# Block maxima and scales of the media for two tiles at once in the first sweep of a gated cross-attention stack

## The chip, the cores and the metric

The kernel runs on one core of one Trainium2 chip. The metric is the device time of one execution in microseconds (us), the median over the runs. A core has five engines that run their own instruction streams and wait for each other through semaphores: TensorE (PE in the profile, its weight loads PEld), VectorE (DVE), ScalarE (ACT), GpSimd (POOL) and SyncE (SP, which here issues the DMAs).

## The reference

Four gated residual layers over x of shape (4, 1024, 1024), with a second input of the same shape, the media (`ctx_2048`). The first layer is the one that the change touches:

```python
def quant_dequant_act_1x128(x):
    E, M, K = x.shape
    xb = x.reshape(E, M, K // BLK, BLK)
    amax = jnp.max(jnp.abs(xb), axis=-1, keepdims=True)
    safe = jnp.maximum(amax, ACT_EPS)
    q = (xb * (FP8_MAX / safe)).astype(jnp.float8_e4m3fn)
    return (q.astype(jnp.float32) * (safe / FP8_MAX)).reshape(E, M, K)

def quant_dequant_weight_128x128(w):
    E, N, K = w.shape
    wb = w.reshape(E, N // BLK, BLK, K // BLK, BLK)
    amax = jnp.max(jnp.abs(wb), axis=(2, 4), keepdims=True)
    safe = jnp.maximum(amax, W_EPS)
    q = (wb * (FP8_MAX / safe)).astype(jnp.float8_e4m3fn)
    return (q.astype(jnp.float32) * (safe / FP8_MAX)).reshape(E, N, K)

xq = quant_dequant_act_1x128(x)
wq = quant_dequant_weight_128x128(weight)
return jnp.einsum('emk,enk->emn', xq, wq)
...
x = x + jnp.tanh(g_xattn[0]) * _L0_xattn_ref(_layernorm(x, axis=-1), ctx_2048)
x = x + jnp.tanh(g_ffn[0]) * _L0_ffn_ref(_layernorm(x, axis=-1), L0_ffn_weight, L0_ffn_norm_weight)
x = x + jnp.tanh(g_xattn[1]) * _L1_xattn_ref(_layernorm(x, axis=-1), ctx_2048, ctx_2048)
x = x + jnp.tanh(g_ffn[1]) * _L1_ffn_ref(_layernorm(x, axis=-1), L1_ffn_router_w, L1_ffn_Wa, L1_ffn_Wb)
```

The media of one batch are the weight matrix of the first layer. They are scaled in blocks of 128 x 128 by the largest magnitude of each block, rounded to the grid of an 8-bit float, and scaled back. The other three layers are a ternary linear layer, an attention over the media with 8 heads, and a mixture of 8 low-rank experts, 2 per token.

## The kernel before

The 4096 rows are 32 tiles of 128 rows (`NT` = 32), 8 to a batch (`TPB`). The **first sweep** (to about 555 us) computes the first layer, writes the sum `x1` to DRAM and gathers what the second layer needs of it. A **second sweep** (to about 1670 us) does the second and third layer and the routing, and a last part runs the experts.

In the first sweep there are two kinds of tiles. A `Rows` tile t holds 128 rows of x. A `Media` tile t holds 128 channels of the media, which are 128 x 1024 numbers: eight blocks of 128 columns side by side. All eight media tiles of a batch make its weight matrix, kept in two halves of 512 outputs (`wqs`, four buffers).

For a media tile these methods run, one after the other, in several steps of the sweep:

- `load` (L253): SP fetches the tile `c` (four buffers).
- `range` (L257): DVE reduces the magnitudes of each block over its columns, 128 x 1024 to 128 x 8 (`rmax`), and PE transposes this to 8 x 128 in PSUM (`rmaxT`).
- `largest` (L266): DVE takes the largest along each of the 8 rows (`top`), puts the eight values on the diagonal of an 8 x 8 matrix (`spot`), and PE multiplies a matrix of ones by it, so that each partition gets all eight block maxima (`bmax`, 128 x 8 in PSUM). One such product in float32 is two passes on PE in the profile.
- `scales` (L276): DVE computes `safe`, its reciprocal, `up` and, for tiles that are not scaled on ACT, `lift`; POOL computes `down`. All are 128 x 8.
- `magnitude` (L289): ACT writes the magnitudes in bfloat16.
- `round` (L296): DVE rounds to the 8-bit grid, with eight operations on 128 x 128 for `k16` (L203), eight for `y` (L208) and one subtraction (L213). In the opening, even tiles are scaled on ACT first (`scale`, L293).
- `store` (L302): ACT and DVE scale back into `wqs`, four blocks each (L237, L241), or seven and one for the first batch.

A `Rows` tile goes through `sum`, `mean`, `square`, `variance`, `range`, `scales`, `scale`, `round`, `restore` (`hd`, L237), `transpose` (eight `ptx` on PE, L375), `take` (`hT`, L381) and `product(0)`, `product(1)` (L388, eight float32 matmuls for each half, which are sixteen rows of the profile), then `residual` (L397), which writes `x1`, `spread`, `factor` and, for some tiles, `extreme` (L426).

The order on PE, DVE, ACT and POOL is the order in which the program is written (`tc.manual_schedule`, L588). SP's order is not written by hand. An **opening** (L589 to L652) prepares the first batch's media, two tiles in each of four rounds, and the first rows. Then `step(t)` (L517) runs for t = 0 to 31. Step t works on several tiles at different depths: `product` of row t, `restore` and `transpose` of row t+1, `scales` and `round` of row t+2, and of the media `store` of tile t+7, `scales` and `round` of tile t+8, `range`, `largest` and `magnitude` of tile t+9, `load` of tile t+11. Media tiles end at 31, so that `largest` runs in steps 0 to 22. In a step PE's order is `product(0)`, `rmaxT`, eight `ptx`, `product(1)`, `bmax`. DVE's is the row scales' reciprocal, the shared part of `store`, `residual` of row t-1, media `range`, media `scales` and `round`, `factor` and `extreme` of row t-2 (even t only, up to step 26), `variance` and `range` of row t+3, `round` of row t+2, and media `top` and `spot`.

The transposed maxima and the spread ones share two PSUM buffers (`ps_r`). From step 23 on, reloads of `x1` and the ternary weights of the second layer are worked in beside the products.

Of the kernel before, what the change touches and what calls it, by code (L numbers as in the profile page):

```python
# [53 lines left out]
def flamingo_kernel(  # L54
# [106 lines left out]
    def cols(k):  # L161
        return slice(k * P, (k + 1) * P)


    with ExitStack() as s1:
# [5 lines left out]

        gamma_2 = wb_sb[:, 6, :]

        ones_8 = w1.tile([NB, P], F32, tag="ones_8", name="ones_8", bufs=1)
        nc.gpsimd.memset(ones_8, 1.0)


        wqs = {}
# [66 lines left out]
        class Media(Fp8):  # L245


            def __init__(self, t):
                self.t, self.name = t, f"w{t}"

                self.scaled = t < TPB and t % 2 == 0
# [3 lines left out]
                nc.sync.dma_start(self.c, vr[self.t])  # L255

            def range(self):  # L257
                rmax = self.tiny("rmax")
                nc.vector.tensor_reduce(
                    rmax, self.c.rearrange("p (b k) -> p b k", k=P), AX.X, ALU.max,  # L260
                    apply_absolute_value=True,
                )
                self.turned = ps_r.tile([NB, P], F32, tag="r", name=f"rmaxT_{self.t}")
                nc.tensor.transpose(self.turned, rmax, ident)

            def largest(self):  # L266


                top = small.tile([NB, 1], F32, tag="topw", name=f"top_{self.name}")
                nc.vector.tensor_reduce(top, self.turned, AX.X, ALU.max)  # L270
                spot = small.tile([NB, NB], F32, tag="spot", name=f"spot_{self.name}")
                nc.vector.tensor_scalar(spot, ident[0:NB, 0:NB], top, None, ALU.mult)
                self.amax = ps_r.tile([P, NB], F32, tag="r", name=f"bmax_{self.t}")
                nc.tensor.matmul(self.amax, ones_8, spot, start=True, stop=True)

            def scales(self):  # L276

                safe = self.tiny("safe")
                nc.vector.tensor_scalar(safe, self.amax, W_EPS, None, ALU.max)
                self.up = self.tiny("up")  # L280
                nc.vector.reciprocal(self.up, safe)
                nc.vector.tensor_scalar(self.up, self.up, FP8_MAX, None, ALU.mult)
                if not self.scaled:
                    self.lift = self.tiny("lift")
                    nc.vector.tensor_scalar(self.lift, self.up, FP8_LIFT, None, ALU.mult)
                self.down = self.tiny("down")
                nc.gpsimd.tensor_scalar(self.down, safe, 1.0 / FP8_MAX, None, ALU.mult)

            def magnitude(self):  # L289
                self.size = w1.tile([P, D], BF16, tag="sizew", name=f"size_{self.name}")  # L290
# [11 lines left out]
            def store(self):  # L302
                b, hf, j = self.t // TPB, self.t % TPB // NH, self.t % NH
                if (b, hf) not in wqs:
                    wqs[b, hf] = wqp.tile([P, NB, HALF], F32, tag="wq", name=f"wq_{b}_{hf}")
                self.dequantize(wqs[b, hf][:, :, cols(j)], 4 if b else 1)

        class Rows(Fp8):

# [171 lines left out]
        rows = [Rows(t) for t in range(NT)]  # L481
        media_t = [Media(t) for t in range(NT)]

        def at(items, t):
            return items[t] if 0 <= t < len(items) else None

# [30 lines left out]
        def step(t):  # L517

            near, new, ahead, far, past, old = (at(rows, t + i) for i in (1, 2, 3, 4, -1, -2))
            mp, m, mr, mn = (at(media_t, t + TPB + i) for i in (-1, 0, 1, 3))
            last = t - (NT - TPB)
            if ahead:
                ahead.mean()
            if new:
                new.scales()
            if t:
                rows[t].product(0)
            if near:  # L530
                near.restore()
            if mp and t:
                mp.store()
            if ahead:
                ahead.square()
            if past:
                past.residual()
            if mr:
                mr.range()
            if new:  # L540
                new.scale()
            if near:
                near.transpose()
                near.take()
            if m:
                m.scales()
                m.round()
            if old:
                old.factor()
                if old not in waiting:  # L550
                    old.extreme()
            if ahead:
                ahead.variance()
                ahead.range()
            if new:
                new.round()
            rows[t].product(1)
            if mr:
                mr.largest()
            if past:  # L560
                past.spread()
            if mr:
                mr.magnitude()
            if far:
                far.sum()
            if at(rows, t + 5):
                rows[t + 5].load()
            if mn:
                mn.load()
            if last >= 0:  # L570
                for r in waiting[2 * last : 2 * last + 2]:
                    r.late_extreme()
            if last >= -1:
                for r in waiting[2 * last + 2 : 2 * last + 4]:
                    r.reload()

            if last in (0, 1):
                load_linear(last)
            if 1 <= last < 5:
                ternary_sum(2 * last - 2)  # L580
                ternary_sum(2 * last - 1)
            if last == 4:
                ternary_scale()
            if 5 <= last:
                for j in range(3 * (last - 5), min(3 * (last - 4), NB)):
                    ternary_block(j)

        with tc.manual_schedule(engines=ORDERED):  # L588
            media_t[0].load()  # L589
            rows[0].load()  # L590
            for i in (1, 2, 3):
                media_t[i].load()
            for r in rows[1:5]:
                r.load()
            media_t[0].range()
            rows[0].sum()
            rows[0].mean()
            rows[0].square()
            media_t[1].range()
            for m in media_t[0:2]:  # L600
                m.largest()
                m.scales()
            media_t[1].magnitude()
            media_t[0].scale()
            rows[0].variance()
            rows[0].range()
            for i in range(TPB // 2):
                m, n = media_t[2 * i : 2 * i + 2]
                nexts = media_t[2 * i + 2 : min(2 * i + 4, TPB + 1)]
                n.round()  # L610
                if i == 0:
                    rows[0].scales()
                    rows[0].scale()
                elif i == 1:
                    rows[1].sum()
                elif i == 2:
                    rows[1].scales()
                    rows[1].scale()
                else:
                    rows[2].sum()  # L620
                n.store()
                nexts[-1].magnitude()
                for j in nexts:
                    j.range()
                if i in (1, 3):
                    rows[(i + 1) // 2].mean()
                    rows[(i + 1) // 2].square()
                m.round()
                m.store()
                for j in range(2 * i + 4, min(2 * i + 6, TPB + 3)):  # L630
                    media_t[j].load()
                for j in nexts:
                    j.largest()
                if i < 3:
                    for j in nexts:
                        j.scales()
                    nexts[0].scale()
                if i == 0:
                    rows[0].round()
                    rows[0].restore()  # L640
                    rows[0].transpose()
                    rows[0].take()
                elif i == 1:
                    rows[1].variance()
                    rows[1].range()
                    rows[0].product(0)
                elif i == 2:
                    rows[1].round()
                else:
                    rows[2].variance()  # L650
                    rows[2].range()
                    rows[3].sum()  # L652
            constants()
            for t in range(NT):
                step(t)
                if t == 3:
                    clear()
            rows[NT - 2].factor()
            rows[NT - 2].extreme()
            first_scale()  # L660
            rows[NT - 1].residual()
            rows[NT - 1].spread()
            rows[NT - 1].factor()
            rows[NT - 1].extreme()
# [988 lines left out]
```

## Time and profile before

| | |
|---|---|
| runs | 2026.25, 2027.53, 2030.4 us; median 2027.53 |
| the profiled execution | 2027.54 us; its span 2025.3 us; mean granted clock of TensorE 0.989 |
| first sweep, steps 1 to 22 (84.63 to 419.67 us) | PE busy 335.04 of 335.04 us, DVE 308.39, ACT 289.25, POOL 127.02 |
| `rmax`, 128 x 8 from 128 x 1024, DVE L259 | 32 times, median 1.209 us |
| `rmaxT`, 128 x 8 transposed, PE L264 | 32 times, median 0.273 us |
| `top`, DVE L270 | 32 times, median 0.272 us |
| `spot`, DVE L272 | 32 times, median 0.219 us |
| `bmax`, PE L274 | 64 passes for 32 products, median 0.272 us |
| `safe`, reciprocal, `up`, `lift`, DVE L279 to L285 | 32, 32, 32 and 28 times, medians 0.156, 0.203, 0.171 and 0.172 us |
| `down`, POOL L287 | 32 times, median 0.233 us |
| media load, SP L255 | 32 times 512 KB, median 3.7 us to landing |

Durations of neighbouring instructions overlap on every engine: from the start of one to the start of the next is often less than its duration. The matmuls' rows above show 0.27 us, though PE starts another one after about 0.11 us.

### The profile page before, as it was taken

The numbers are of one execution on the slowest core, as the hardware profiler recorded it, in microseconds if no ns is written. First come the engines' busy times: TensorE is split into PE (matmuls) and PEld (weight loads), VectorE is DVE, ScalarE is ACT, GpSimd is POOL, SyncE is SP. The second block draws the span as 40 slices with busy tenths as digits, with TensorE's granted clock in tenths as the row PEclk, the third lists the DMA queues.
The fourth block names the chain that finished last, engine by engine and source line by source line (L and its number), as shares of the span: only waits on it lengthen the run. The fifth ranks groups of instructions, "written<-read, shape, count | busy, mean of one in ns | idle before, by whom it ended". The sixth has DMA issues, their size and how long they took to land.

```text
span 2025.3 us, 25153 instructions
## 1 busy us (share of the span) xinstructions
PE 1919.7 (95%) x7232; PEld 998.3 (49%) x7264; DVE 1682.9 (83%) x3527; ACT 1436.2 (71%) x2410; POOL 601.8 (30%) x930
## 2 busy tenths in 40 slices
PE   3599999999879999999999999999999989999998
PEld 1244444444324444444444444444444447777776
DVE  8999999988778999999999999999999846555555
ACT  7988888888457777777777777777777645555554
POOL 2233433433100212121212121211121235646664
PEclk9799999999989999999999999999999999999999
DMA  4143233263186677767777767677767765856985
GB/s 176 64 156 104 94 115 105 94 208 115 42 244 165 177 198 177 199 178 196 179 199 178 198 177 199 177 199 177 199 177 187 209 185 183 286 171 197 311 297 175
DMA packets 124751, 357.77 MB, mean 177 GB/s; under 512 B 30583, under 2 KB 38775, under 8 KB 124614
## 3 DMA queue, kind: packets, MB, share of 16 engines
q1 hardware_dynamic: 95094, 271.78, 49.1%
q0 software_dynamic: 29520, 84.39, 12.4%
q8 instruction: 58, 0.95, 0.2%
q14 instruction: 79, 0.65, 0.1%
HBM read 164.08 MB, written 75.61 MB: 118 GB/s over the span
## 4 chain that ended last, share of the span: by engine, by line
PE 84%; DVE 6%; issue 4%; DMA 2%; ACT 2%; POOL 2%; SPq 0%; POOLq 0%; DVEq 0%; ACTq 0%
PE sc L843 21%; PE av L923 21%; PE mm L388 20%; PE f L804 5%; PE dn L1389 5%; PE up L1399 4%; PE pt_hmT L971 1%; PE ptx L375 1%; PE pt_hg_pt L1360 1%; PE pq L983 1%; PE pt_hg_acc L1360 1%; DVE nmax L848 1%; ACT e L852 1%; PE ptq L796 1%; DMA eT_x<-sq 1%
## 5 line engine op out<-in xcount | busy, mean ns | idle before, releaser
L843 PE MATMUL sc<-kv,q 128*128 128x512 f32 x1024 | 488.9, 600 | 4.3 <-ACT q L831 2.6
L923 PE MATMUL av<-eT_x,vT 128*128 128x512 f32 x1008 | 477.4, 596 | 4.4 <-DMA eT_x<-sq 1.8
L388 PE MATMUL mm<-wq,hT 128*128 128x512 f32 x1024 | 453.8, 597 | 0.0
L852 ACT ACTIVATE e<-sc,nmax 128x1024 f32<-128x1024 f32 x256 | 285.4, 1115 | 229.9 <-DVE nmax L848 227.0
L848 DVE TENSOR_REDUCE nmax<-sc 128x1 f32<-128x1024 f32 x256 | 311.9, 1218 | 45.4 <-PE sc L843 45.2
L858 ACT ACTIVATE e<-e,rden 128x1024 f32<-128x1024 f32 x256 | 294.2, 1149 | 58.9 <-DVE rden L855 52.7
L871 DVE STREAM_TRANSPOSE sq<-e 128x1024 f32<-128x1024 f32 x252 | 310.9, 1234 | 0.1
L923 PEld LDWEIGHTS av<-eT_x,vT 128*128 128x128 f32 x1008 | 189.1, 190 | 233.8 <-issue 230.2
L388 PEld LDWEIGHTS mm<-wq,hT 128*128 128x128 f32 x1024 | 191.2, 191 | 220.3 <-issue 216.4
L843 PEld LDWEIGHTS sc<-kv,q 128*128 128x128 f32 x1024 | 185.0, 191 | 188.0 <-issue 175.1
L1389 PEld LDWEIGHTS dn<-hgT,arena_w 128*128 128x128 f32 x1216 | 147.1, 192 | 43.7 <-issue 33.4
L1389 PE MATMUL dn<-hgT,arena_w 128*128 128x128 f32 x1216 | 149.8, 277 | 6.4 <-DVE arena_w L1373 4.7
L133 POOL TENSOR_TENSOR rstd_c<-ve_c,neg_half 128x1 f32<-128x1 f32 x31 | 17.7, 570 | 461.3 <-DVE nrm L998 405.3
L1399 PE MATMUL up<-arena_w,ygT 128*128 128x512 f32 x304 | 143.1, 594 | 0.0
L804 PE MATMUL f<-wb_sb 128*128 128x512 bf16 x465 | 115.4, 379 | 4.2 <-DVE y L812 1.4
L1394 ACT COPY ygT<-dn 128x128 f32<-128x128 f32 x76 | 20.3, 267 | 135.5 <-PE dn L1389 132.5
L225 ACT ACTIVATE y_x<-x,off_x,up_x 128x128 f32<-128x128 f32 x256 | 101.5, 480 | 11.5 <-POOL off_x L357 11.5
L237 ACT ACTIVATE hd<-q_x,down_x 128x128 f32<-128x128 bf16 x256 | 78.1, 388 | 21.8 <-DVE q_x L213 21.6
L804 PEld LDWEIGHTS <-wb_sb 128*128 128x128 bf16 x496 | 48.5, 98 | 81.6 <-issue 29.4
L1073 POOL DMA_INDIRECT lists<-token,slot x64 | 66.7, 1042 | 67.4 <-DVE slot L1066 56.8
L133 POOL TENSOR_TENSOR a_all<-va,neg_half 128x1 f32<-128x1 f32 x32 | 36.2, 1131 | 153.1 <-DVE va L417 95.0
L133 POOL TENSOR_TENSOR y<-ve_d,neg_half 128x1 f32<-128x1 f32 x32 | 18.4, 574 | 212.7 <-issue 161.8
(297 smaller groups left out, 2933.7 us busy)
## 6 DMA issues: line engine op xcount, KB each, us to landing
eT_x<-sq SPq DMA_DIRECT2D x1008, 128.0 KB, 2.4
x<-y SPq DMA_DIRECT2D x32, 514.0 KB, 3.5
c<-in_ctx_t_dram SPq DMA_DIRECT2D x32, 512.0 KB, 3.7
x<-in_x_dram SPq DMA_DIRECT2D x32, 512.0 KB, 4.5
x<-x1s SPq DMA_DIRECT2D x32, 512.0 KB, 2.9
y<-x SPq DMA_DIRECT2D x32, 512.0 KB, 4.6
kv<-in_ctx_dram SPq DMA_DIRECT2D x32, 512.0 KB, 4.6
vT<-in_ctx_t_dram SPq DMA_DIRECT2D x32, 512.0 KB
```

What stands on the lines that cost most here:

```text
L225: nc.scalar.activation(self.y[:, cols(k)], src[:, cols(k)], AF.Identity, bias=bias[:, k : k + 1], scale=scale[:, k : k + 1],)
L237: nc.scalar.activation(dst[:, k, :], self.q[:, cols(k)], AF.Copy, scale=down)
L388: nc.tensor.matmul(self.pm[:, hf * HALF : (hf + 1) * HALF], self.hT[:, k, :], wq[:, k, :], start=(k == 0), stop=(k == NB - 1),)
L804: nc.tensor.matmul(po, self.qT[:, k, :], w0T[:, k, cols], start=(k == 0), stop=(k == NB - 1),)
L843: nc.tensor.matmul(sc[:, halves(nh)], qs[t][:, mb * P : (mb + 1) * P], kv[:, halves(nh)], start=True, stop=True,)
L848: nc.vector.tensor_reduce(nmax, sc, AX.X, ALU.max, negate=True)
L852: nc.scalar.activation(self.e, sc, AF.Exp, bias=nmax, accum_out=self.den)
L858: nc.scalar.activation(self.e, self.e, AF.Copy, scale=self.rden)
L871: nc.vector.transpose(sq[:, :, :, j, :], self.e.rearrange("p (k q a) -> p q k a", k=NB, q=4))
L923: nc.tensor.matmul(out_ap, vTs[t][:, k, :], weights, start=(k == 0), stop=(k == NB - 1))
L1389: nc.tensor.matmul(po, self.wa[:, k, :], self.hT[:, k, :], start=(k == 0), stop=(k == NB - 1),)
L1399: nc.tensor.matmul(po[:, halves(hf)], self.yT, self.wb[:, halves(hf)], start=True, stop=True)
```

## The change

Media tiles get a `Group`: tiles 0 and 1 one each, and from tile 2 on two neighbouring tiles. The maxima over columns of both tiles go into one tile of 128 x 16, by two reductions; `turn` transposes it once, right behind the second reduction; `largest` and `scales` run once for the group, on 16 columns. Each tile then reads its eight columns of `up`, `lift` and `down`.

In the steps, tile t+10 instead of t+9 is reduced, the group is turned and spread in odd steps, and `scales` runs in even steps, for tiles t+8 and t+9. `magnitude` stays with tile t+9 and keeps its place. In the opening's last round the maxima of tiles 8 and 9 are taken instead of that of tile 8 alone. `lift` is computed for all tiles, also for the scaled ones of a group. The small tiles of the groups lie in another pool, `w1`, with three buffers as before.

```diff
-        ones_8 = w1.tile([NB, P], F32, tag="ones_8", name="ones_8", bufs=1)
-        nc.gpsimd.memset(ones_8, 1.0)
+        ones_16 = w1.tile([2 * NB, P], F32, tag="ones_16", name="ones_16", bufs=1)
+        nc.gpsimd.memset(ones_16, 1.0)
...
             def range(self):
-                rmax = self.tiny("rmax")
+                g = self.group
                 nc.vector.tensor_reduce(
-                    rmax, self.c.rearrange("p (b k) -> p b k", k=P), AX.X, ALU.max,
+                    g.column(g.rmax, self), self.c.rearrange("p (b k) -> p b k", k=P), AX.X, ALU.max,
                     apply_absolute_value=True,
                 )
-                self.turned = ps_r.tile([NB, P], F32, tag="r", name=f"rmaxT_{self.t}")
-                nc.tensor.transpose(self.turned, rmax, ident)
...
+                if self is g.tiles[-1]:
+                    g.turn()
+
+            @property
+            def up(self):
+                return self.group.column(self.group.up, self)
...
+        class Group:
+
+
+            def __init__(self, tiles):
+                self.tiles, self.n = tiles, NB * len(tiles)
...
+            def tiny(self, name):
+                return w1.tile([P, 2 * NB], F32, tag=f"{name}w", name=f"{name}_w{self.name}", bufs=3)[
+                    :, 0 : self.n
+                ]
+
+            def column(self, of, m):
+                i = self.tiles.index(m)
+                return of[:, i * NB : (i + 1) * NB]
+
+            def begin(self):
+                self.rmax = self.tiny("rmax")
+
+            def turn(self):
+                self.turned = ps_r.tile([2 * NB, P], F32, tag="r", name=f"rmaxT_{self.name}")
+                nc.tensor.transpose(self.turned[0 : self.n, :], self.rmax, ident)
+
+            def largest(self):
+
+
+                n = self.n
+                top = small.tile([2 * NB, 1], F32, tag="topw", name=f"top_w{self.name}")
+                nc.vector.tensor_reduce(top[0:n, :], self.turned[0:n, :], AX.X, ALU.max)
+                spot = small.tile([2 * NB, 2 * NB], F32, tag="spot", name=f"spot_w{self.name}")
+                nc.vector.tensor_scalar(spot[0:n, 0:n], ident[0:n, 0:n], top[0:n, :], None, ALU.mult)
+                self.amax = ps_r.tile([P, 2 * NB], F32, tag="r", name=f"bmax_{self.name}")
+                nc.tensor.matmul(
+                    self.amax[:, 0:n], ones_16[0:n, :], spot[0:n, 0:n], start=True, stop=True
+                )
+
+            def scales(self):
+
+                safe = self.tiny("safe")
+                nc.vector.tensor_scalar(safe, self.amax[:, 0 : self.n], W_EPS, None, ALU.max)
+                self.up = self.tiny("up")
+                nc.vector.reciprocal(self.up, safe)
+                nc.vector.tensor_scalar(self.up, self.up, FP8_MAX, None, ALU.mult)
+                self.lift = self.tiny("lift")
+                nc.vector.tensor_scalar(self.lift, self.up, FP8_LIFT, None, ALU.mult)
+                self.down = self.tiny("down")
+                nc.gpsimd.tensor_scalar(self.down, safe, 1.0 / FP8_MAX, None, ALU.mult)
...
+        groups = [Group(media_t[i : i + 1]) for i in (0, 1)]
+        groups += [Group(media_t[i : i + 2]) for i in range(2, NT, 2)]
...
-            mp, m, mr, mn = (at(media_t, t + TPB + i) for i in (-1, 0, 1, 3))
+            mp, m, mr, ms, mn = (at(media_t, t + TPB + i) for i in (-1, 0, 2, 1, 3))
...
             if mr:
+                if t % 2 == 0:
+                    mr.group.begin()
                 mr.range()
...
             if m:
-                m.scales()
+                if t % 2 == 0:
+                    m.group.scales()
                 m.round()
...
             rows[t].product(1)
-            if mr:
-                mr.largest()
+            if mr and t % 2:
+                mr.group.largest()
             if past:
                 past.spread()
-            if mr:
-                mr.magnitude()
+            if ms:
+                ms.magnitude()
...
-                nexts = media_t[2 * i + 2 : min(2 * i + 4, TPB + 1)]
+                nexts = media_t[2 * i + 2 : 2 * i + 4]
...
-                nexts[-1].magnitude()
+                nexts[-1 if i < 3 else 0].magnitude()
+                nexts[0].group.begin()
                 for j in nexts:
                     j.range()
...
-                for j in nexts:
-                    j.largest()
+                nexts[0].group.largest()
                 if i < 3:
-                    for j in nexts:
-                        j.scales()
+                    nexts[0].group.scales()
                     nexts[0].scale()
```

More of the change, by code (lines that the diff above doesn't have):

```diff
@@ L257, in range, with lift, down @@
             def range(self):
-                rmax = self.tiny("rmax")
+                g = self.group
                 nc.vector.tensor_reduce(
-                    rmax, self.c.rearrange("p (b k) -> p b k", k=P), AX.X, ALU.max,
+                    g.column(g.rmax, self), self.c.rearrange("p (b k) -> p b k", k=P), AX.X, ALU.max,
                     apply_absolute_value=True,
                 )
-                self.turned = ps_r.tile([NB, P], F32, tag="r", name=f"rmaxT_{self.t}")
[L264 to L287, printed above, removed]
+                if self is g.tiles[-1]:
[3 more added lines that the diff above has]
+                return self.group.column(self.group.up, self)
+            @property
+            def lift(self):
+                return self.group.column(self.group.lift, self)
+            @property
+            def down(self):
+                return self.group.column(self.group.down, self)
             def magnitude(self):
@@ L306, in store @@
                 self.dequantize(wqs[b, hf][:, :, cols(j)], 4 if b else 1)
+        class Group:
+            def __init__(self, tiles):
+                self.tiles, self.n = tiles, NB * len(tiles)
+                self.name = "_".join(str(m.t) for m in tiles)
+                for m in tiles:
+                    m.group = self
+            def tiny(self, name):
[30 more added lines that the diff above has]
+                nc.gpsimd.tensor_scalar(self.down, safe, 1.0 / FP8_MAX, None, ALU.mult)
         class Rows(Fp8):
@@ L594, in flamingo_kernel @@
                 r.load()
+            for g in groups[0:2]:
+                g.begin()
             media_t[0].range()
@@ L599, in flamingo_kernel @@
             media_t[1].range()
-            for m in media_t[0:2]:
-                m.largest()
-                m.scales()
+            for g in groups[0:2]:
+                g.largest()
+                g.scales()
             media_t[1].magnitude()
```

## The prediction

> **What bounds the kernel now.** I read the page first (busy shares and slices), then the chain of waits in order of time over the first 680 us, then busy time by stretch for single steps, then the timeline of two neighbouring steps and of the first 100 us, and last the DMA queue of SP.
>
> ```profile
> PE 1919.7 (95%) x7232; PEld 998.3 (49%) x7264; DVE 1682.9 (83%) x3527; ACT 1436.2 (71%) x2410; POOL 601.8 (30%) x930
> PE   3599999999879999999999999999999989999998
> PEclk9799999999989999999999999999999999999999
> ```
>
> One digit is 50.6 us. The first sweep fills the first eleven. TensorE (PE) is idle a good part of the first 80 us and then not at all until after 500 us. The chain says the same: vector work until 84 us, then only `mm`, `ptx`, `mm`. The stretches are one step of the sweep each:
>
> ```profile
> 252.15:267.38 15.23, 15.23 (x45) 7.17 (x44) 14.47 (x43) 11.46 (x26) 5.64 (x6) 1.00 0.32 105
> 267.38:282.61 15.23, 15.23 (x45) 7.17 (x44) 13.44 (x41) 14.80 (x38) 5.74 (x10) 1.00 0.33 104
> 442.12:456.73 14.61, 14.61 (x42) 6.91 (x41) 11.66 (x20) 10.96 (x26) 3.85 (x7) 1.00 0.63 223
> ```
>
> The columns are the stretch, its length, then busy time of PE, weight loads, VectorE (DVE), ScalarE (ACT) and POOL, the granted clock, the DMA share and GB/s. The first two are steps 12 and 13, the third is step 25. PE is busy for the whole of each, at clock 1.00. What steps 12 and 13 have on PE and step 25 has not is the media's work: 45 matmuls against 42, and 0.62 us. The timeline of step 12 shows where it sits:
>
> ```profile
> 259.12 0.27 PE L264 MATMUL rmaxT<-ident,rmax_w 128*8 128x128 f32 x1
> 259.23 1.04 PE L375 MATMUL ptx<-ident,hd 128*128 128x128 f32 x8
> 260.10 7.03 PE L388 MATMUL mm<-wq,hT 128*128 128x512 f32 x16
> ...
> 266.25 0.22 DVE L272 TENSOR_SCALAR spot_w<-ident,top_w 8x8 f32<-8x8 f32 x1
> ...
> 267.07 0.38 PE L274 MATMUL bmax<-spot_w,ones 8*128 8x8 f32 x2
> ...
> 267.38 7.13 PE L388 MATMUL mm<-wq,hT 128*128 128x512 f32 x16
> ```
>
> From start to start: `rmaxT` 0.11, the two passes of `bmax` 0.31, and the sixteen `mm` ahead of each 6.97 where 6.87 is found without them (half of 13.73 in step 25): 0.11 + 0.31 + 0.20 = 0.62 us. Step 1 starts at 84.63 and step 23 at 419.67, so 22 steps take 335.04, or 15.229 each; steps without media take 14.61.
>
> **The change in the steps.** Before, step t transposes the maxima of media tile t+9 and spreads their block maxima; after, step t reduces tile t+10, the transpose comes in odd steps only, for two tiles, and so does `bmax`. Of steps 1 to 22, the eleven even ones lose both: 11 x (15.229 - 14.61) = 6.8 us off PE. The eleven odd ones keep both, with 16 columns. `rmaxT` streams 128 columns as before; only its weight load doubles in width (0.087 us at 8 columns, 0.141 in the `ptx` row at 128, and `ptx` still follows one another every 0.11), so 0 to 0.03. `bmax` streams 16 columns for 8; at 0.43 us for 512 columns that is 0.007 a pass, and the floor is nothing. I take 0.02 a step, 0.2 us in all (bounds 0 to 0.5).
>
> On DVE a pair of tiles saves `top`, `spot`, `safe`, the reciprocal and two products: by pitch 0.31 + 0.14 + 0.19 + 0.24 + 0.20 + 0.20 = 1.3 us, less the widening (0.156 us for 128x8 at L279, 0.24 for 128x32 at L685: about 0.03 for eight more columns, over four of them 0.1). POOL saves one 0.23 us product. I count none of this as time: PE covers it. That cover holds if DVE, after the change, still ends inside PE's 14.61 + 15.23 = 29.84 us for a pair:
>
> ```profile
> 282.40 1.28 DVE L397 SCALAR_TENSOR_TENSOR x1s<-mm,tg,x 128x1024 f32<-128x1024 f32 x1 [1.49 <-PE mm L388]
> ```
>
> This is the residual that opens the next step on DVE; the residual of step 12 starts at 251.94. So DVE needs 30.46 - 1.49 = 28.97 us for the pair now, and 28.97 - 1.2 = 27.8 after, with 2.0 to spare. Unevenly: even steps hold `extreme` and now all the `scales`, and last 15.39 - 0.45 = 14.9 against PE's 14.61. The odd residual then starts some 0.4 us late. Its reader on PE is the product that reuses its PSUM tile, a whole step away, and the odd step, lighter by 0.8, catches up. What the change adds as a wait is light too: `bmax` waits for `spot`, which in the tight even steps is ready 0.6 us ahead of PE (266.47 against 267.07); there it vanishes, and in odd steps it is ready at 279.97 for 282.30.
>
> ACT does the same work in the same places. Its idle time over the pair is 1.79 + 0.36 + 1.60 + 0.34 = 4.1 us, each behind PE or DVE, and the pair shortens by 0.62. PE waits for ACT at `ptx`: `hd` of step 12 ends at 268.57, `ptx` starts at 274.46, so 5.9 us of cover shrink to 5.3.
>
> **The SP queue.** No DMA is added, but the load of a media tile is now read one step earlier.
>
> ```profile
> 268.63 0.33 SPq L400 DMA_DIRECT2D x<-x1s  x1
> 269.01 0.43 SPq L316 DMA_DIRECT2D x<-in_x_dram  x1
> 274.23 0.33 SPq L255 DMA_DIRECT2D c<-in_ctx_t_dram  x1
> ```
>
> The load at 274.23 in step 13 is that of tile 25 (13 loads are out by 79 us, then one a step). It lands 3.7 us later (median) and was read in step 16; now in step 15, from about 298 us. Twenty microseconds of cover remain: nothing.
>
> **The opening.** Up to step 0 DVE sets the time. For a pair the six small operations and their twins run from 24.27 to 26.71, 2.44 us, and the second tile's `top` and `spot` fill the wait for the first `bmax`. After, the wait shows: tile 0 alone has `spot` ending at 9.48 and `safe` starting at 10.23, 0.75. So 0.30 + 0.22 + 0.75 + 0.80 + 0.1 for width = 2.2 us, 0.25 saved, in three pairs 0.75 (bounds 0 to 1.2). Against it the maximum of tile 9 moves from step 0 into the opening: one more reduction at 1.17. Net 0.4 later into step 0 (bounds 0 to 1.2). Step 0 itself, though, is even:
>
> ```profile
> 84.04 0.22 DVE L272 TENSOR_SCALAR spot_w<-ident,top_w 8x8 f32<-8x8 f32 x1
> 84.32 0.38 PE L274 MATMUL bmax<-spot_w,ones 8*128 8x8 f32 x2 [0.67 <-DVE mu_a L324]
> 84.63 7.13 PE L388 MATMUL mm<-wq,hT 128*128 128x512 f32 x16
> ```
>
> PE has finished row 0's product at 83.65 and waits 0.67 us for `spot`, then spends 0.31. Both go: 0.98. The first `mm` of step 1 needs only `hT` of row 1, ready at 81.70. The product itself starts at 76.20, held by eight `ptx` that stood behind a `rmaxT` until 74.32 with `hd` running since 73.02; without it up to 0.4 comes back, of which I take 0.2. So 0.98 - 0.4 + 0.2 = 0.8 us gained. One price is unsure, the clock. The stretch from 50 to 75 us was granted 0.63, and the sixteen `mm` from 41.88 took 9.16 us where the ones at 76.20 took 7.45. Were the latter as slow, 1.7 would be lost; but `ptx` and `mm` of step 0 follow each other as before, so I take zero. Bounds of the opening: from 0.8 - 0.8 - 1.7 = -1.7 to 1.4.
>
> A rule of the Trainium skill speaks to that price: "TensorE: Matmul & The Clock Gate", Part 1, has the array at half its clock until about 3.4 us of sustained work have passed, and back there after an idle window as long. By it the two matmuls taken out of step 0 could leave one window more at half clock, an estimated 1.7 us from the page's figures, and the sum below would be 5.7; the row at 41.88, slow for its first five pairs and then not, agrees with the rule, but no row here shows step 0 with fewer matmuls ahead.
>
> **Sum.** 6.8 - 0.2 + 0.8 = 7.4 us. The profiled execution took 2027.54 (span 2025.3, 2.24 around it), which is the median of the runs, 2027.53. 2027.54 - 7.4 = **2020.1**. Nothing after 420 us is touched; from step 24 to 500 us PE runs at 14.61 a step with no gap, so what follows it moves forward whole. Its first gap, near 507 us, waits for ACT and DVE work that itself starts from that step's products.
>
> **Rivals.**
> *Given back by ACT.* In odd steps ACT is busy 14.80 of 15.23. If it could not take up the shorter even step, PE would stand in the odd one for the 0.62 saved, and only the opening's 0.8 would stay: 2026.7. For it speaks the 14.80; against it the 3.77 idle in even steps and 5.9 us ahead of `ptx`.
> *DVE was the bound.* If PE only looked full, the sweep would fall by DVE's 1.2 a pair, 11 x 1.2 + 0.8 = 14.0: 2013.5. Even steps, with DVE idle only 0.45 inside, speak for it; the 1.49 of every odd step spent waiting for `mm` against.
> *The maximum waits for its media.* SP's order is not written by hand; this rival has the load queued in the very step that reads it, behind the store of `x1` and the row load. Then the reduction, next on DVE after the residual, waits 0.33 + 0.43 + 3.7 = 4.5 us a step; behind it stand `scales`, both roundings and `spot`, and PE waits for those. A pair would be DVE's: 27.8 + 9.0 = 36.8 against 30.46, 11 x 6.3 less 0.8, or 2096. It decides once a load lands after the residual: under 4.5 us before it, where the queue now shows over 20. Against it is also that four buffers free the place a step before.
> *Not doing what it says:* if `bmax` of 16 columns took as long as two of 8, 11 x 0.41 is lost of 7.4: 2024.6. The 512-column rows say otherwise.
>
> **How the numbers follow.** About 0.2% (4.1 us) is what a measurement here can tell from no change, so faster means under 2023.5 and slower over 2031.6. The forecast has 0.82; with its bounds (6.8 - 0.5 - 1.7 = 4.6 to 6.8 + 1.4 = 8.2) it runs from 2019.3 to 2022.9, and with 1.3 for runs (the fastest stands that far below the median) from 2018.0 to 2024.2. ACT's rival has 0.09, the wide `bmax` 0.02, DVE's 0.03, the late media 0.04. The range is the forecast's own; what lies outside is 0.18 of rivals at most. Faster 0.82 + 0.03 = 0.85, same 0.09 + 0.02 = 0.11, slower 0.04.
>
> **What the changed profile would show.** Even steps of 14.6 with 42 matmuls and no `rmaxT` or `bmax`; odd ones of 15.2 with `128*16` and `16x16`; 11 fewer of each transpose in the steps; step 1 starting near 83.8 and step 23 near 412; DVE's idle before the odd residual near zero and before the even one near 2; everything from there on the same lengths as before. Even steps that stay at 15.2, a DVE wait for `DMA c`, or a second sweep of another length would prove it wrong.

## The result and the profile after

The changed kernel took 2017.64 us (median of 6 runs, 2015.36 to 2020.57), the kernel before in the same series 2027.82 (6 runs, 2025.75 to 2031.34). The ratio is 0.9947, interval 0.9937 to 0.9957: faster by 0.53%, or 10.7 us (8.7 to 12.8); the medians themselves lie 10.2 us apart. The profiled execution is the slowest of the six, 2020.57 us with a span of 2018.8, 6.5 us under the span before.

From the page after, busy shares and two rows of slices:

```profile
span 2018.8 us, 24982 instructions
PE 1915.2 (95%) x7219; PEld 994.8 (49%) x7219; DVE 1670.1 (83%) x3441; ACT 1433.4 (71%) x2410; POOL 595.2 (29%) x915
PE   3599999999889999999999999999999989999998
PEclk9799999999999999999999999999999999999999
```

DVE has lost 86 instructions and POOL 15. PE is as full as it was. Steps 12 (even) and 13 (odd) by stretch, with the columns of the stretches before:

```profile
247.46:262.07 14.61, 14.61 (x41) 7.01 (x41) 13.72 (x38) 10.84 (x23) 5.21 (x6) 1.00 0.33 108
262.07:277.30 15.23, 15.23 (x44) 7.07 (x42) 13.26 (x39) 15.20 (x40) 5.76 (x10) 1.00 0.30 105
```

The even step is now as short as a step without media, the odd one as long as before. PE is busy for the whole of both. The timeline of step 13 shows the wide pair of instructions, 16 columns each:

```profile
269.04 0.27 PE L320 MATMUL rmaxT<-ident,rmax_w 128*16 128x128 f32 x1
269.15 1.04 PE L414 MATMUL ptx<-ident,hd 128*128 128x128 f32 x8
270.02 7.03 PE L427 MATMUL mm<-wq,hT 128*128 128x512 f32 x16
276.98 0.39 PE L331 MATMUL bmax<-spot_w,ones 16*128 16x16 f32 x2
277.30 0.70 PE L427 MATMUL mm<-wq,hT 128*128 128x512 f32 x1
```

From start to start `rmaxT` takes 0.11 us and `bmax` 0.32, against 0.11 and 0.31 at 8 columns: the width costs about 0.01. On DVE, the residuals that open steps 12 and 13, in the same timeline:

```profile
247.25 1.28 DVE L436 SCALAR_TENSOR_TENSOR x1s<-mm,tg,x 128x1024 f32<-128x1024 f32 x1 [1.57 <-PE mm L427]
...
262.48 1.28 DVE L436 SCALAR_TENSOR_TENSOR x1s<-mm,tg,x 128x1024 f32<-128x1024 f32 x1
```

The first waits 1.57 us for PE; the second, behind the heavier even step, not at all, and nothing on PE waits for it. The opening and step 0, again in order of time:

```profile
68.67 0.27 DVE L327 TENSOR_REDUCE top_w<-rmaxT 16x1 f32<-16x128 f32 x1
68.98 0.22 DVE L329 TENSOR_SCALAR spot_w<-ident,top_w 16x16 f32<-16x16 f32 x1
...
69.25 0.60 PE L331 MATMUL bmax<-spot_w,ones 16*128 16x16 f32 x2 [3.30 <-DVE ve_a L374]
...
73.04 2.52 PE L414 MATMUL ptx<-ident,hd 128*128 128x128 f32 x8 [3.19 <-ACT hd L237]
...
75.35 14.78 PE L427 MATMUL mm<-wq,hT 128*128 128x512 f32 x32
...
90.08 1.04 PE L414 MATMUL ptx<-ident,hd 128*128 128x128 f32 x8
```

The products of step 0 and of step 1 now follow each other, 32 matmuls in one row, where `bmax` and its wait for `spot` stood at 84.32. Step 1's `ptx` start at 90.08 instead of 91.71, step 23's at 418.26 instead of 426.64.

To see where the rest of the time goes, the traces of both kernels are cut at instructions that both have. The runs "again" and "third" are those of the next section; "first `k16`" is the start of tile 1's rounding, "experts" runs from the first `dn` to the end. The two runs "again" were on one chip, number 7, and "third" on another, number 3; which chip the plain "before" and "changed" ran on is not known.

| us | first `k16` | `ptx` of step 1 | to `ptx` of step 23 | experts | span |
|---|---|---|---|---|---|
| before | 13.86 | 91.71 | 334.93 | 353.9 | 2025.3 |
| before, again | 13.59 | 92.02 | 334.93 | 360.0 | 2033.7 |
| changed | 13.24 | 90.08 | 328.18 | 356.3 | 2018.8 |
| changed, again | 13.22 | 91.36 | 328.19 | 360.2 | 2025.0 |
| changed, third | 14.12 | 92.22 | 328.18 | 360.6 | 2025.6 |

The steps are exact to 0.01 us, and 6.75 us shorter. The experts' part is the same code in all five and moves by 6.7 us. From step 23's `ptx` to the end of the span it is 1598.7 and 1606.7 us before and 1600.5, 1605.4 and 1605.2 changed, so the traces show no steady gain behind the steps.

### The profile page after: what moved, and what is told of

The parts are those of the page before. It is cut to its first block, busy times and chain, and to the rows that moved or that the text cites. A ratio compares the mean times of both kernels' runs of the same rounds, so it can differ in the third digit from the quotient of the medians.

```text
span 2018.8 us, 24982 instructions
## 1 busy us (share of the span) xinstructions
PE 1915.2 (95%) x7219; PEld 994.8 (49%) x7219; DVE 1670.1 (83%) x3441; ACT 1433.4 (71%) x2410; POOL 595.2 (29%) x915
## 4 chain that ended last, share of the span: by engine, by line
PE 83%; DVE 6%; issue 4%; POOL 2%; ACT 2%; DMA 1%; SPq 0%; POOLq 0%; DVEq 0%; ACTq 0%
PE sc L890 21%; PE av L970 21%; PE mm L427 21%; PE f L851 5%; PE dn L1436 4%; PE up L1446 4%; PE pt_hmT L1018 1%; PE ptx L414 1%; PE pq L1030 1%; PE pt_hg_pt L1407 1%; ACT e L899 1%; DVE nmax L895 1%; PE pt_hg_acc L1407 1%; PE ptq L843 1%; POOL arena_x L1383 1%
```

## The experiments

**Both kernels again.** No edit.

> The changed kernel once more, unaltered. Theory (all of the gain is the first sweep's 8.4 us, as the two traces show it up to the first product after the ternary transpose; what lies behind varies from run to run): ratio to before 0.9959 or 8.4 us, step 1 to step 23 again 328.2 us between ptx starts, and the later parts again some us longer or shorter than in the first trace. Rival (the change also shortens what follows the sweep by about 2 us): ratio 0.9947 or 10.2 us again, and a trace whose second sweep or expert part is shorter than both before's.

> The kernel before, unaltered, for a second trace and for the noise. Both theories: ratio 1.000. If the 0.6 us by which the second media tile came earlier in the changed kernel's opening is a matter of the run, this trace shows the second block reduction starting somewhere between 7.0 and 7.8 us; if it belongs to the change, at 7.8 again. Experts' part: 353.9 us again if it is fixed by the code, otherwise off by a us or two.

> The changed kernel a third time, timed beside the version of this call. Theory: 7.9 us of the first sweep and nothing else, ratio 0.996, whatever the chip; the rival that it gains more elsewhere wants 0.9947 again.

Measured: the changed kernel's ratio was 0.9963 (interval 0.995 to 0.9975; medians 2026.9 against 2033.98) and, the third time, 0.9966 (0.9954 to 0.9978; 2030.98 against 2038.05); 12 runs of the changed kernel each time. That is 7.5 us (5.1 to 10.2) and 6.9 us (4.5 to 9.4). The kernel before against itself gave 0.9996 (0.9979 to 1.0013). The second block reduction of the kernel before started at 7.54 us this time, against 7.82, and in four traces with the changed opening at 6.98, 6.99, 7.52 and 7.82: how early the first DMAs land is a matter of the run. The rival, a gain behind the sweep, wanted 10.2 again and a shorter experts' part; it got neither.

**PE's share put back.**

```diff
+            back = media_t[t + TPB].group if t in range(2, NT - TPB, 2) else None
+            if back:
+                back.turn_again()      # transpose of the group's rmax into ps_r
...
+            if back:
+                back.spread_again()    # ones_16 times the group's spot into ps_r
```

> The changed kernel with PE's share put back alone: in each even step from 2 to 22 the group's transpose and its product of ones are done a second time on PE at the old places, into PSUM that nobody reads; DVE keeps its savings. Theory (PE sets the step): even steps back to 15.23, 11 x 0.62 = 6.8 us slower than the changed kernel, about 2024.5, ratio to before 0.998. Rival (DVE's smaller load made the steps shorter): no change against the changed kernel, 2017.6.

Measured: ratio 0.9999 (0.9982 to 1.0016). By stretch, from step 1's `ptx` to step 23's, and step 12:

```profile
91.43:426.51 335.08, 335.08 (x948) 157.79 (x946) 297.44 (x826) 289.15 (x662) 123.00 (x168) 1.00 0.32 112
256.60:271.83 15.23, 15.23 (x44) 7.17 (x43) 14.48 (x40) 11.00 (x26) 5.82 (x7) 1.00 0.31 108
```

335.08 us is the length before, with DVE's busy time (297.44) that of the changed kernel, not the 308.25 that the kernel before has over these steps. PE alone, in even steps alone, gives back 6.9 us. The time came back further than the 0.998 that was expected, which lies just outside the interval; the steps came back as expected.

**DVE's share put back**, once and three times.

```diff
                 if t % 2 == 0:
                     m.group.scales()
+                else:
+                    for i in range(1):      # range(3) in the second kernel
+                        m.group.scales_again(i)
...
+            if t in range(2, NT - TPB, 2):
+                for i in range(1):
+                    media_t[t + TPB].group.largest_again(i)
```

> The changed kernel with DVE's share put back alone: in each odd step the four scale operations, in each even one top and spot are done a second time on DVE into tiles that nobody reads; PE keeps its savings. Theory: DVE has 1.6 to 2.0 us to spare in a pair of steps and gets about 1.4 more work, so the steps stay at 29.84 a pair, 2017.6 within noise, and DVE's idle time ahead of the residual falls to 0.2 to 0.6. Rival (DVE sets the step): 11 x 1.4 = 15 us slower, 2033.

> As the run with DVE's share put back, but three times over: some 4.2 us of small operations more in each pair of steps. Theory (1.6 to 2.0 us of a pair are to spare on DVE): 2.2 to 2.6 us a pair too much, so 11 pairs cost 24 to 29 us, the pair 32.1 to 32.4 us, and PE idles in the steps. Rival (the trace's idle time understates DVE's cover, other waits move too): no change, 2018 to 2027 by the chip.

Measured, once: ratio 0.996 (0.9944 to 0.9976). From step 1's `ptx` to step 23's:

```profile
90.63:418.82 328.19, 328.19 (x915) 154.86 (x913) 308.54 (x895) 290.31 (x666) 124.31 (x166) 1.00 0.33 113
```

DVE is as busy again (308.54 us) as in the kernel before, and the steps stay at 328.19. The waits of DVE between 90 and 400 us (what waits, for what: us in total, times, longest), first in the changed kernel, then in this one:

```profile
DVE x1s L436 <- PE mm L427: 15.4, 11, 1.6
DVE amax_all L468 <- POOL a_all L133: 4.5, 10, 0.5
DVE mu_a L363 <- ACT wb_sb L359: 2.3, 10, 0.3
DVE inv_x L393 <- POOL amax_x L386: 1.6, 10, 0.2
```

```profile
DVE x1s L453 <- PE mm L444: 7.5, 9, 0.9
DVE amax_all L485 <- POOL a_all L133: 4.5, 10, 0.5
```

The added work went into the wait: 15.4 + 2.3 + 1.6 - 7.5 = 11.8 us over eleven pairs, 1.1 a pair, and 0.7 a pair are left ahead of the residual where 0.2 to 0.6 were expected. All that DVE can give is (15.4 + 2.3 + 1.6) / 11 = 1.75 us a pair. Three times: step 23's `ptx` came 345.4 us behind step 1's, 17.2 us late, or 1.6 a pair; one execution took 2037.2 us beside one of 2025.21 for the kernel before. PE over one pair's time, in the changed kernel and then in this one:

```profile
300.00:329.84 29.84, 29.84 (x85) 14.07 (x84) 26.98 (x76) 26.02 (x61) 10.96 (x16) 1.00 0.33 107
```

```profile
300.00:329.84 29.84, 28.40 (x81) 13.41 (x80) 28.98 (x90) 24.77 (x58) 10.10 (x15) 1.00 0.28 100
```

Now PE is the one with gaps. 3 x 1.1 - 1.75 = 1.55 us a pair agrees with the 1.6; the 24 to 29 us expected were too many because the price of one copy, 1.4, was.

**Only the transpose put back.** The edit of the PE run without `spread_again`.

> The changed kernel with only the second transpose put back on PE in the even steps from 2 to 22; the product of ones stays halved. Read in the trace. Theory (each of the two costs PE its own slot and 0.10 us of the sixteen matmuls ahead of it): even steps 14.61 + 0.21 = 14.82 us, 22 steps of the sweep 11 x 0.21 = 2.3 us longer than the changed kernel's 328.2. Rival (the two-pass product costs all of it): 328.2 again; or (the transposes cost all of it) 335.

Measured: 329.39 us for the 22 steps, 1.2 more than changed, or 0.11 for each of the eleven even steps. Half of what was expected. The timeline of an even step:

```profile
248.06 0.39 PE L332 MATMUL bmax<-spot_w,ones 16*128 16x16 f32 x2
248.38 7.13 PE L439 MATMUL mm<-wq,hT 128*128 128x512 f32 x16
255.35 0.27 PE L338 MATMUL rmaxG<-ident,rmax_w 128*16 128x128 f32 x1
255.46 1.04 PE L426 MATMUL ptx<-ident,hd 128*128 128x128 f32 x8
256.33 13.90 PE L439 MATMUL mm<-wq,hT 128*128 128x512 f32 x32
270.07 0.27 PE L320 MATMUL rmaxT<-ident,rmax_w 128*16 128x128 f32 x1
```

The sixteen `mm` behind `bmax` take 6.97 us, and the 32 that reach up to the next `rmaxT` 13.74, no more than without one. A transpose beside other transposes costs its slot of 0.11. The 0.20 that the prediction shared out between the two belongs to `bmax`, which cuts a row of `mm` in two: 0.31 + 0.20 = 0.51 us each time.

**The opening one by one.**

```diff
-        groups = [Group(media_t[i : i + 1]) for i in (0, 1)]
-        groups += [Group(media_t[i : i + 2]) for i in range(2, NT, 2)]
+        groups = [Group(media_t[i : i + 1]) for i in range(TPB)]
+        groups += [Group(media_t[i : i + 2]) for i in range(TPB, NT, 2)]
```

(with a loop over the groups in the opening, and no `lift` for a scaled tile alone)

> The changed kernel with the opening's tiles 2 to 7 one by one again; tiles 8 and 9 and all later ones stay paired. Read in the trace. Theory (three pairs save 0.25 to 0.3 us each, because the wait for the product of ones shows): DVE from the first k16 of tile 1 to the last q of the opening takes 0.8 us longer than in the changed kernel, and step 1's ptx come 0.8 us later, give or take the clock's phase in step 0 (16 matmuls there have taken 7.45 to 8.7 us). Rival (the pairs of the opening bring nothing, the reduction of tile 9 is hidden): no difference.

Measured: from the first `k16` to the last `q` of the opening 54.90 us, against 53.97 in the changed kernel and 53.76 in the kernel before. The three pairs save 0.93 us, and tile 9's reduction costs a little more than that; net, DVE gets out of the opening 0.2 us later. The first `mm` of step 0 came 63.04 us behind the first `k16`, 62.11 in the changed kernel: the same 0.93. Step 1's `ptx` came 78.66 us behind the first `k16`, in seven kernels with the changed opening 76.44 to 78.14 (mean 77.17), in the two of before 77.85 and 78.43. The steps were 328.19.

**PE kept warm.**

```diff
                 nexts[0].group.largest()
+                if i == 3:
+                    ghost = ps_r.tile([P, P], F32, tag="r", name="ghost")
+                    for _ in range(14):
+                        nc.tensor.transpose(ghost, ident, ident)
```

> The changed kernel with 14 transposes of the identity on PE behind the opening's last product of ones, into PSUM that nobody reads: about 3.1 us of PE work at half clock where PE idles from 69.9 to 73.0. Theory (the products of step 0 start at a low clock because PE idled before them, and by how much is a matter of phase): the first 32 matmuls take 13.9 to 14.2 us where runs of the changed kernel took 14.5 to 16.05, and step 1's ptx come 0.5 to 2 us earlier. Rival (they are slow for another reason, such as late weights): still 14.5 to 16 us.

Measured: 75.98 us from the first `k16` to step 1's `ptx`, less than in any of those seven, and 14.15 us for the 32 matmuls. The stretches from their start to 83 or 84.5 us (PE, weight loads, DVE, ACT, POOL, then the granted clock), first of this kernel, then of the changed one in its first trace and in the run "again":

```profile
76.05:83.00 6.95, 6.95 (x17) 3.19 (x17) 6.85 (x19) 6.92 (x15) 2.18 (x2) 0.96 0.24 77
```

```profile
75.35:83.00 7.65, 7.65 (x17) 3.37 (x17) 7.55 (x19) 7.62 (x15) 2.77 (x3) 0.88 0.21 70
```

```profile
75.36:84.50 9.14, 9.14 (x18) 3.93 (x18) 8.87 (x25) 8.84 (x20) 3.91 (x4) 0.76 0.18 58
```

Nearly the same instructions were granted 0.96, 0.88 and 0.76. Step 0's length is a matter of the clock, and in both kernels: the sixteen `mm` of the kernel before took 7.45 us in its first trace and 8.75 in the second. In each trace the granted clock goes from 0.50 to 1.00 at one moment of step 0. In the changed kernel's first trace this is at 77.12 us, and the two stretches from step 0's `ptx` to that moment, and from there to step 1's `ptx`, are:

```profile
73.04:77.12 4.08, 4.08 (x11) 2.28 (x12) 3.94 (x18) 4.08 (x12) 0.89 (x4) 0.50 0.00 0
77.13:90.08 12.95, 12.95 (x33) 5.67 (x32) 12.65 (x35) 12.64 (x31) 4.43 (x6) 1.00 0.36 124
```

The moment came 0.98 to 4.33 us behind the first of the 32 matmuls in the seven kernels with the changed opening, and each microsecond of delay cost half a microsecond: 14.39 us at 0.98, 16.05 at 4.33. In the kernel with the fourteen transposes it came at 0.50 us. That is one execution, 0.24 us under the shortest of the seven, so that the transposes did it is not shown.

**A version from these findings.** Tile 9's reduction behind the last rounding, row 2's variance and range ahead of `largest`, and eleven transposes where PE idles.

```diff
-                for j in nexts:
+                for j in nexts[: 2 if i < 3 else 1]:
                     j.range()
...
+                if i == 3:
+                    nexts[1].range()
+                    ghost = ps_r.tile([P, P], F32, tag="r", name="ghost")
+                    for _ in range(8):
+                        nc.tensor.transpose(ghost, ident, ident)
+                    rows[2].variance()
+                    rows[2].range()
                 nexts[0].group.largest()
+                if i == 3:
+                    for _ in range(3):
+                        nc.tensor.transpose(ghost, ident, ident)
```

> A version built from the findings: the reduction of tile 9 goes behind the opening's last rounding, with row 2's variance and range ahead of the group's largest, so that ACT and PE get row 1 sooner; and eleven transposes of the identity run on PE where it idles ahead of step 0. Theory: the last q of the opening comes 1.1 us earlier against the first k16, step 0's 32 matmuls take 13.9 to 14.2 us, and step 1's ptx come 1.5 to 2 us earlier against the first k16 than in the changed kernel (75.0 us behind it instead of 76.4 to 78.1), steps 1 to 23 unchanged at 328.2; in all 2 us, ratio about 0.995. Rival (DVE's chain, which is as long as before, holds step 1 back): no gain, ratio as the changed kernel's.

> The same without the eleven transposes. Read in the trace. Theory: last q 1.1 us earlier against the first k16, step 1's ptx 75.3 to 77.0 us behind it, by the clock's phase. Rival as in the run before.

Measured: ratio 0.9941 (0.9922 to 0.9959) beside 0.9966 (0.9954 to 0.9978) for the changed kernel in the same series: below it, but the two intervals overlap, and the 3.8 us between the medians (2027.15 and 2030.98) are more than the traces account for. The traces are surer. The last `q` came 52.85 us behind the first `k16` (52.82 without the transposes), 1.1 earlier, as expected. Step 1's `ptx` came 75.90 behind it, 76.50 without the transposes, so 1.3 and 0.7 us before the changed kernel's mean; the first `mm` of step 0 came 61.00 and 60.97 behind it, 1.1 us before the changed kernel's 62.11, whatever the clock did after. The steps kept 328.19. The clock was a miss:

```profile
69.61 1.91 PE L685 MATMUL ghost<-ident 128*128 128x128 f32 x8
...
71.99 0.90 PE L691 MATMUL ghost<-ident 128*128 128x128 f32 x3
...
72.68 2.37 PE L414 MATMUL ptx<-ident,hd 128*128 128x128 f32 x8
...
74.85 14.96 PE L427 MATMUL mm<-wq,hT 128*128 128x512 f32 x32
```

The 32 matmuls took 14.96 us, not 13.9 to 14.2. The clock rose 2.13 us behind the first of them, within the range of the seven kernels without transposes. With one trace of eleven transposes spread over 3.3 us and one of fourteen in a row, whether either moves that moment stays open.

## Why the prediction was right in its mechanism and short in its size

**The steps: right.** Predicted 6.8 - 0.2 = 6.6 us off the 22 steps, measured 6.75. That PE sets them is shown from both sides: PE's work put back takes all of it away, DVE's takes nothing. The split was wrong, as the transpose run shows: 0.11 + 0.51, not 0.21 + 0.41.

**DVE as cover: right, with wrong figures that cancelled.** 2.0 us to spare became 1.75; a copy of the small operations costs 1.1 a pair, not 1.3. The even steps ran past PE, the odd ones caught up, as foreseen. Neither ACT nor the SP queue added a wait: in odd steps ACT is busy 15.20 of 15.23 and PE still does not wait for it, and between 90 and 400 us DVE never waits for a media load.

**The opening: too small by 0.2 us on average, and by 0.8 in the first pair of traces.** Predicted 0.8, seen in the first traces 91.71 - 90.08 = 1.63. Of that 0.62 is the first DMAs' landing (13.86 against 13.24), which is the run's; counted from the first `k16`, the seven traces of the changed opening lie 1.0 us before the two of before. The pairs saved 0.93 for 0.75. The first `mm` of step 0 came 62.11 us behind the first `k16` for 62.34 in the first traces, so 0.23 earlier, where the sum had it 0.2 later (0.4 less 0.2). The clock, which I set to zero, makes up to 1.7 us of difference in the changed step 0: 14.39 to 16.05 us for the same 32 matmuls. It also decides whether the 0.67 us of waiting for `spot` are there to be gained. In the second trace of the kernel before, where the clock rose late, they are not:

```profile
75.95 8.75 PE L388 MATMUL mm<-wq,hT 128*128 128x512 f32 x16
84.63 0.38 PE L274 MATMUL bmax<-spot_w,ones 8*128 8x8 f32 x2
```

Two traces of the kernel before are few for an average, so the 1.0 is rough. The row at 41.88 was misread too: not five pairs but five of its sixteen matmuls are slow, 0.85 to 1.01 us from start to start against 0.43 to 0.45.

The Trainium skill, "TensorE: Matmul & The Clock Gate", Part 1, has the array slow until a window of about 3.4 us has been busy, with windows that do not start with the kernel. The traces agree with it: up to step 0, the stretches at one granted clock last 6.83, 10.24, 20.48, 23.89 or 27.31 us, all multiples of 3.41. That the change itself would leave PE cold for longer, as the prediction weighed by that page, is not seen: the clock rose 0.98 to 4.33 us behind step 0's first matmul in the seven traces of the changed opening, and 0.84 and 3.45 us in the two of before.

**The step that failed: the 1.3 us for runs.** The forecast's own end at low times was 6.8 + 1.4 = 8.2 us under the profiled execution, and "with 1.3 for runs (the fastest stands that far below the median) from 2018.0". The median came at 2017.64, 0.36 outside. I took the spread from three runs in one place and laid the whole forecast on one profiled execution. What the runs showed in its place: in the three timed series the fastest run stood 1.6 to 4.8 us below its kernel's median, not 1.3. The experts' part, untouched by the change, took 350.6 to 362.4 us over the eleven traces of the experiments and the two first ones, and differed by 1.8 to 3.5 us between traces of one series. Its level goes with the series, each of which ran on one chip: 356.7 to 360.2 us on chip 7, 350.6 to 353.8 on chip 6, 360.6 to 362.4 on chip 3; chip and hour cannot be told apart here.

The same kernel before read 2027.8, 2034.0 and 2038.1 in the three timed series, the last two on chips 7 and 3, and the difference between the two kernels 10.7, 7.5 and 6.9 us. The first sweep accounts for 6.75 + 1.0 = 7.7 of it, inside the intervals of the second and third series and 1 us outside that of the first. In the experts' part the waits on PE differ from trace to trace. Between 1675 and 2015 us, what PE's `dn` waited for in the changed kernel "again", and in the run with the opening one by one, whose experts were the quickest:

```profile
PE dn L1436 <- ACT hgT L1411: 7.1, 5, 3.5
PE dn L1436 <- issue: 3.2, 2, 2.6
```

```profile
PE dn L1441 <- DVE arena_w L1425: 3.4, 3, 1.7
PE dn L1441 <- ACT hg L1395: 0.2, 1, 0.2
```

10.3 us against 3.6, in the same code, though on two chips. That the first series drew such luck for the changed kernel in its unprofiled runs is likely, not shown: those runs left no trace, and the one that did lost 2.4 us in that part. So it stays open whether about 1 us of the first 10.7 has another source.

**The rivals.** ACT giving the gain back, DVE as the bound, the wide `bmax` at double price and the late media load are all refuted by the rows above: even steps at 14.61, DVE's load put back for nothing, 0.32 us for 0.31, no wait for a load.

## What to carry to other kernels

On an engine that is busy all of the time, count what a small instruction costs from the start of the last large one ahead to the end of the next one behind: a two-pass product in the middle of a row of matmuls cost 0.51 us here, a transpose among transposes 0.11. Halving the number of such instructions pays by the step, at 16 columns for 8 here (no wider one was tried), as long as the cover of the other engines is counted for the longest period in which they must catch up. A range needs the spread of every later part of the program, across several executions, and not only the bounds of the terms in the sum.

## What was not expected of the hardware

Sixteen columns cost PE 0.01 us more than eight (0.32 against 0.31 for `bmax`). On DVE, `safe`, `up` and `lift` of 128x16 took 0.17 us each as at 128x8, and the reciprocal 0.25 for 0.20. The granted clock in one short step moved the same 32 matmuls by 1.7 us between executions of kernels that did the same work ahead of it: it rose from 0.50 to 1.00 at one moment, 0.98 to 4.33 us behind the first of them.
